# Gate and up products of six blocks by Strassen's scheme

## The chip, the cores and the metric

The kernel runs on one core of a Trainium2 chip. The metric is the device time of one execution in microseconds (us). Engine names: PE is TensorE (matmuls; PEld its weight loads), DVE is VectorE, ACT is ScalarE, POOL is GpSimd, SP is SyncE, which here only issues DMAs.

## The reference

`x` has 4 sequences of 1024 tokens with 512 channels, all in f32. One layer norm feeds two branches, and both are added to `x`:

```python
xn = _layernorm(x, axis=-1)
x = x + attn(xn, ...) + ffn(xn, w_gate, w_up, w_down)

def ffn(x, w_gate, w_up, w_down):
    gate = jnp.einsum('bsd,hd->bsh', x, w_gate)      # hidden width 2048
    up = jnp.einsum('bsd,hd->bsh', x, w_up)
    gated = jax.nn.silu(gate) * up
    return jnp.einsum('bsh,dh->bsd', gated, w_down)
```

The attention branch is an RMS norm, q, k and v by ternary weights, a causal linear attention with decay over chunks of 128 tokens (16 heads of 32, a running state `S` of 32x32 per head), two RMS norms and a ternary projection.

## The kernel before

The 4096 tokens are 8 blocks of 512. Every f32 operand of a large product is split into a high and a low f16 part, and a product is three matmuls: high by high, high by low, low by high. A matmul has a 128x128 weight tile and up to 512 moving columns.

**FFN.** `x` is normed and transposed into `xT` (high and low, 4 channel tiles of 128 rows, 512 token columns). The 2048 hidden units are 16 tiles `j`. For each `j`, `ffn_up` (L681) makes gate and then up: 4 channel tiles by 3 matmuls of 512 columns each, into one PSUM bank of the pool `ps_f` (3 banks). ACT applies Silu to gate (L693); DVE multiplies up by it and by a scale (L696); ACT casts to f16 (L699), and POOL or DVE subtracts for the low part (L700), giving `ghl`. Eight `j`s are a half `hh`; after them `ffn_down` (L704) makes the down products of four token chunks `k`, 24 matmuls each, and `add_acc` (L719) adds them to `acc`, which was loaded from `x`. Two `j`s share one scale, and are called a group or a pair.

The weights are scaled, split and stored to `gu_d` in DRAM while block 1 runs (`ffn0` with `stage`, `group_conv` L342). Later blocks load a 512 KB tile `gu` per `j` from there (L736; 4 buffers).

**Norm of the next block.** `ln_stats` computes mean and variance; `ln` (L430) splits four chunks of 128 tokens into high and low (ACT cast L436, POOL subtraction L437) and turns each by a DMA transpose into `xT` (L438).

**Attention.** `att_half` (L458) handles 256 tokens. It makes q and k (16 matmuls of 256 columns for each of four parts, tiles `wqkT` and `h`), sends them through DRAM (`sd`) into the layouts `qst` and `kst`, and turns k by a transpose into `kn`. Then follow v, and per chunk and quarter `qd` of the heads: `scores` (4 matmuls into the single bank of `ps_s`; DVE masks, L545; ACT casts, L547; POOL subtracts, L548), `intra` two steps later, `cross`, `state`, `norms`, and `proj`, which also ends in `add_acc`.

**Order.** `ffn0` and `ffn` are generators with 48 steps a block. After each step the main loop (L848 on) runs one step of the preparation `side` and `side2`, `make_h` (L444; the attention's own norm weight) where it is due, and one step of every attention half in flight. Halves start at steps 36 + 22.4 n (L841). PE keeps the program's order (`tc.keep_in_program_order`, L74); the order on the other engines and in SP's queue is set by the framework when the kernel is built. The attention's f32 temporaries and the FFN's share the tag `t32` (9 buffers of 512 columns).

## Time and profile before

Three runs took 1366.82, 1367.73 and 1367.89 us (median 1367.73). The profiled execution took 1368.61 us, of which 1366.7 are the span from the first to the last instruction.

| engine | busy us | share of the span |
|---|---|---|
| PE | 1322.6 | 97% |
| PEld | 695.6 | 51% |
| DVE | 719.9 | 53% |
| POOL | 619.6 | 45% |
| ACT | 550.3 | 40% |
| DMA queue of SP | | 47% of 16 engines |

In the profile, "psf<-xT,gu" means that the tile psf is written and xT and gu are read; "<-POOL gu L360" behind idle time names what ended it. A line number is that of the kernel; since every matmul is recorded by one helper, all matmuls have L74, and they are told apart by tiles. A PE row with 1.58 us and x13 is a run of thirteen matmuls; their modelled ends overlap the next run, so that a pitch is read from starts.

### The profile page before, as it was taken

The page shows a single profiled execution, that of the slowest core. Times are in us where ns is not written, and L with a number is a line of the kernel's source. Part 1 is how long each engine was busy: PE and PEld are TensorE (multiplying, and loading weights), DVE is VectorE, ACT ScalarE, POOL GpSimd, SP SyncE. Part 2 cuts the span into 40 slices and gives each one's busy share as a digit, 9 for nine tenths or more (in the row PEclk, how much of TensorE's full clock was granted, in tenths as well). Part 3 has the DMA queues.
Part 4 walks back from the last instruction along what each step waited for, and adds up shares of the span by engine and source line. Part 5 has one row for each costly group of instructions (what it writes and reads, how often), then busy time and mean ns, then how long its engine had stood idle before and what let it go on. Part 6 is the DMA issues. An engine that isn't in the chain of part 4 may idle for free.

```text
span 1366.7 us, 21760 instructions
## 1 busy us (share of the span) xinstructions
PE 1322.6 (97%) x8514; PEld 695.6 (51%) x8514; DVE 719.9 (53%) x1415; ACT 550.3 (40%) x1033; POOL 619.6 (45%) x603
## 2 busy tenths in 40 slices
PE   5998989999999999999999999999999999999998
PEld 2443445554555545455455545555555555565554
DVE  7897764445544354453644446453553445356444
ACT  6754443343433334333334243342424334244341
POOL 3657672444624254353634246342545245255451
PEclk9999999999999999999999999999999999999999
DMA  9833836146261554426363354626283444535420
GB/s 343 294 124 114 231 101 180 48 137 156 87 191 31 165 128 125 140 59 173 94 155 108 103 141 104 178 69 162 80 181 95 116 116 106 142 109 124 105 66 31
DMA packets 155974, 178.11 MB, mean 130 GB/s; under 512 B 101600, under 2 KB 101600, under 8 KB 155872
## 3 DMA queue, kind: packets, MB, share of 16 engines
q1 hardware_dynamic: 155728, 176.73, 47.0%
q8 instruction: 66, 1.08, 0.3%
q14 instruction: 36, 0.29, 0.1%
q10 hardware_dynamic: 144, 0.01, 0.0%
HBM read 119.55 MB, written 33.55 MB: 112 GB/s over the span
## 4 chain that ended last, share of the span: by engine, by line
PE 79%; DVE 7%; POOL 7%; issue 3%; DMA 3%; ACT 1%; SPq 0%; POOLq 0%; ACTq 0%; DVEq 0%
PE psf L74 58%; PE psa L74 19%; PE pss L74 2%; DMA xin<-in_x_dram 2%; DMA xT<-xn 1%; POOL t L548 1%; DVE acc L720 1%; POOL xn L437 1%; DVE t L696 1%; DVE gs L312 1%; POOL rs L396 1%; POOL wd L360 1%; DVE t L239 0%; POOL ghl L700 0%; POOL gu L360 0%
## 5 line engine op out<-in xcount | busy, mean ns | idle before, releaser
L74 PE MATMUL psf<-xT,gu 128*128 128x512 f16 x3072 | 703.4, 381 | 10.6 <-POOL gu L360 5.5
L74 PEld LDWEIGHTS <-gu 128*128 128x128 f16 x3072 | 294.7, 98 | 338.0 <-issue 10.1
L74 PE MATMUL psf<-wd,ghl 128*128 128x512 f16 x1536 | 352.3, 380 | 2.7 <-ACT t L693 1.1
L74 PEld LDWEIGHTS <-ghl 128*128 128x128 f16 x1536 | 146.9, 98 | 164.3 <-issue 3.3
L548 POOL TENSOR_TENSOR t<-t,t 128x512 f16<-128x512 f32 x128 | 149.5, 1168 | 164.2 <-ACT t L547 163.9
L700 POOL TENSOR_TENSOR ghl<-t,ghl 128x512 f16<-128x512 f32 x86 | 102.6, 1193 | 163.4 <-ACT ghl L699 150.2
L696 DVE SCALAR_TENSOR_TENSOR t<-psf,bsc,t 128x512 f32<-128x512 f32 x128 | 95.9, 749 | 121.2 <-PE psf L74 104.8
L699 ACT CAST ghl<-t 128x512 f16<-128x512 f32 x128 | 79.0, 617 | 176.1 <-DVE t L696 175.6
L545 DVE SCALAR_TENSOR_TENSOR t<-pss,rs,mask 128x512 f32<-128x512 f32 x128 | 95.3, 744 | 77.2 <-PE pss L74 74.7
L693 ACT ACTIVATE t<-psf,ug 128x512 f32<-128x512 f32 x128 | 87.5, 684 | 98.0 <-PE psf L74 96.6
L74 PE MATMUL psa<-h,wqkT 128*128 128x256 f16 x1024 | 122.2, 273 | 0.0
L519 POOL TENSOR_TENSOR t<-t,t 128x512 f16<-128x512 f32 x28 | 32.6, 1163 | 195.3 <-ACT t L518 195.3
L547 ACT CAST t<-t 128x512 f16<-128x512 f32 x128 | 79.1, 618 | 101.9 <-DVE t L545 96.3
L74 PEld LDWEIGHTS <-wqkT 128*128 128x128 f16 x1024 | 99.7, 98 | 23.4
L720 DVE SCALAR_TENSOR_TENSOR acc<-psf,c,acc 128x512 f32<-128x512 f32 x56 | 41.8, 747 | 63.0 <-PE psf L74 62.7
L74 PEld LDWEIGHTS <-t 128*128 128x128 f16 x1040 | 47.6, 97 | 35.0 <-POOL t L548 3.4
L74 PE MATMUL psa<-wvT,h 128*128 128x512 f16 x256 | 60.5, 379 | 0.0
L74 PE MATMUL pss<-qst,kst 96*128 96x128 f16 x512 | 49.2, 218 | 8.7 <-DVE t L545 6.5
L74 PE MATMUL psa<-wpT,vhl 128*128 128x512 f16 x240 | 56.7, 379 | 0.0
L620 POOL TENSOR_TENSOR vhl<-t,vhl 128x512 f16<-128x512 f32 x30 | 34.7, 1155 | 48.0 <-ACT vhl L619 48.0
L573 POOL TENSOR_TENSOR t<-t,t 128x512 f32<-128x512 f32 x28 | 36.1, 1288 | 44.1 <-DVE t L572 18.6
L508 DVE SCALAR_TENSOR_TENSOR vhl<-psa,rs,vhl 128x512 f16<-128x512 f32 x32 | 24.0, 749 | 56.2 <-ACT vhl L507 54.5
(188 smaller groups left out, 1340.8 us busy)
## 6 DMA issues: line engine op xcount, KB each, us to landing
gu<-gu_d SPq DMA_DIRECT2D x112, 512.0 KB, 3.6
qst<-sd SPq DMA_DIRECT2D x48, 256.0 KB, 4.8
kst<-sd SPq DMA_DIRECT2D x48, 256.0 KB, 4.7
xin<-in_x_dram SPq DMA_DIRECT2D x32, 256.0 KB, 3.0
acc<-in_x_dram SPq DMA_DIRECT2D x32, 256.0 KB, 2.8
gu_d<-gu SPq DMA_DIRECT2D x16, 512.0 KB, 4.1
sd<-qhl SPq DMA_DIRECT2D x16, 512.0 KB, 2.6
sd<-khl SPq DMA_DIRECT2D x16, 512.0 KB, 3.3
```

The lines of the kernel that those rows point to most:

```text
L74: tc.keep_in_program_order(nc.tensor.matmul(*a, **k))
L519: G.tensor_tensor(vrl, vr, vrh, ALU.subtract)
L545: V.scalar_tensor_tensor(sm, pss, u.rk, mask[:, 4 * qd : 4 * qd + 4, :], ALU.mult, ALU.mult)
L547: A.copy(u.smh, sm)
L548: G.tensor_tensor(u.sml, sm, u.smh, ALU.subtract)
L573: G.tensor_tensor(u.o, u.o, oc, ALU.add)
L620: G.tensor_tensor(on[:, 1, :], u.o3, on[:, 0, :], ALU.subtract)
L693: pa = A.activation(sl, pm, AF.Silu, scale=ug[:, j // 2 : j // 2 + 1])
L696: pv = V.scalar_tensor_tensor(gf, pm, bs[:, j // 2 : j // 2 + 1], sl, ALU.mult, ALU.mult)
L699: A.copy(ghl[:, 0, :], gf)
L700: E.tensor_tensor(ghl[:, 1, :], gf, ghl[:, 0, :], ALU.subtract)
L720: V.scalar_tensor_tensor(acc[g], ps, c, acc[g], ALU.mult, ALU.add)
```

## The change

Blocks 1 and 2 keep the plain products. In blocks 3 to 8 gate and up of one pair of hidden tiles are made together as a 2 by 2 block product in seven block products in place of eight (Winograd's form of Strassen's scheme). The two rows are up and gate; the two halves of the inner dimension are channels 0 to 255 and 256 to 511 (u1, u2, g1, g2); the two columns are the token halves of the block (x11, x21 for tokens 0 to 255; x12, x22 for the rest).

- Weight sums S1 = g1 + g2, S2 = S1 - u1, S3 = u1 - g1, S4 = u2 - S2 are made once by `comb`, in steps 50 to 86 (block 2), from weights that `load_comb` loads again, and stored to `gs_d`.
- Sums of x, T1 = x12 - x11, T2 = x22 - T1, T4 = x21 - T2, T3 = x22 - x12, are made by `ln` on POOL in the place of x's own rows, before the split and the transposes. There are seven split parts a block for four. `make_h` gets x12 back as T1 + x11.
- `Pair` makes the products p1 to p7. Each loads a 256 KB weight tile (`gu_tile`, 8 buffers) and has twelve matmuls of 256 columns (two hidden tiles by two channel tiles by three). p1, p6, p7 and p4 accumulate into one bank, which is read after p1, p6 and p7 as well; p5 and p3 share another; p2 has its own.
- `ffn` has again 48 steps a block. p4 and p3 of a pair stand behind p1 and p6 of the next. The down products of a half begin before the last pair's p4 and p3.

Besides: `XS` is 2^9 and not 2^10, and other scales follow; weights are stored by kind and channel half; q and k go to DRAM and to the transpose in quarters and not in halves (tag `qk`, 3 buffers); `acc` has 6 buffers and not 8, with its loads at steps 11 and 15 of a block; `t32` has 10; the projection weights are prepared right behind the qkv weights, one step of preparation for each step of the loop; `ln` runs over seven steps from the 40th of a block; `ln0` has copies of 256 columns in place of 512.

```diff
 RMS_EPS = 1.1920928955078125e-07
-XS = 2.0**10
+XS = 2.0**9
 QS = 2.0**-4
...
-    gu_d = dram.tile([P, NJ * 2048], F16, tag="gu_d", name="gu_d")
+
+
...
     def t32():
-        return wt([P, 512], F32, "t32", 9)
+        return wt([P, 512], F32, "t32", 10)
+    def gu_tile():
+        return wt([P, 2, 2, 2, P], F16, "gu", 8)
+
+    def xq_tile():
+        return wt([P, 2, 2, 2, UT], F16, "xq", 3)
...
 
-    HOLD = {"qst": (4, 1), "kst": (4, 1), "qhl": (2, 1), "khl": (2, 1)}
...
+    def load_comb(k):
+        g, r = divmod(k, 2)
+        for kind in range(2):
+            raw[g, kind, r] = t = wt([P, C], F32, *(("xin", 4) if k < 10 else ("xn2", 2)))
+            SY.dma_start(t, w_gu[2 * g + r, kind])
+
+    def comb(k):
+
+        g, r = divmod(k, 2)
+        sc = []
+        for kind in range(2):
+            src = raw.pop((g, kind, r))
+            A.activation(src, src, AF.Copy, scale=om[:, g, kind : kind + 1])
+            sc += [src[:, :256], src[:, 256:]]
+        g1, g2, u1, u2 = sc
+        ta, tb = t32(), t32()
+        G.tensor_tensor(ta[:, :256], g1, g2, ALU.add)
+        G.tensor_tensor(ta[:, 256:], ta[:, :256], u1, ALU.subtract)
+        G.tensor_tensor(tb[:, :256], u1, g1, ALU.subtract)
+        G.tensor_tensor(tb[:, 256:], u2, ta[:, 256:], ALU.subtract)
+        st = xq_tile().rearrange("p a b c t -> p (a b c t)").rearrange("p (s n q) -> p s n q", s=4, n=2)
+        for n, t in enumerate((ta, tb)):
+            tv, sn = t.rearrange("p (a q) -> p a q", a=2), st[:, 2 * n : 2 * n + 2]
+            A.copy(sn[:, :, 0], tv)
+            V.tensor_tensor(sn[:, :, 1], tv, sn[:, :, 0], ALU.subtract)
+        SY.dma_start(gs_d[:, g, :, r], st.rearrange("p s n q -> p s (n q)"))
 
...
+    def staged(src):
+
+        xn2 = wt([P, 2, 2, UT], F16, "xn2", 2)
+        A.copy(xn2[:, :, 0], src)
+        G.tensor_tensor(xn2[:, :, 1], src, xn2[:, :, 0], ALU.subtract)
+        return xn2
...
     def ln(b):
         rs, xts = lnst.pop(b)
-        xT = wt([P, 2, CC, HB], F16, "xT", 1)
-        blk[b] = [xT, None, rs]
-        for k in range(4):
-            xn2 = wt([P, 2 * C], F16, "xn2", 2).rearrange("p (a c) -> p a c", a=2)
-            A.copy(xn2[:, 0, :], xts[k])
-            G.tensor_tensor(xn2[:, 1, :], xts[k], xn2[:, 0, :], ALU.subtract)
-            SY.dma_start_transpose(
-                xT[:, :, :, k * P : (k + 1) * P].rearrange("p a c t -> p (a c) t"),
-                xn2.rearrange("p a c -> p (a c)"),
+        xq = [None] * 7
+        blk[b] = [xq, None, rs]
+
+        def unit(tile, src, k):
+            xn2 = staged(src)
+            turned(
+                tile[:, :, :, :, k * P : (k + 1) * P].rearrange("p s n c t -> p (s n c) t"),
+                xn2.rearrange("p s n c -> p (s n c)"),
             )
-            yield
+
+        def pair(tiles, qs):
+            t = xq_tile()
+            xq[qs[0]], xq[qs[1]] = t[:, 0], t[:, 1]
+            for k in range(2):
+                unit(t, tiles[k].rearrange("p (s c) -> p s c", s=2), k)
+                yield
+
+        xa, xb = xts[:2], xts[2:]
+        yield from pair(xa, (X11, X21))
+        t2 = t32().rearrange("p (k c) -> p k c", k=2)
+        for k in range(2):
+            T1, x21, x12, x22 = xa[k][:, :256], xa[k][:, 256:], xb[k][:, :256], xb[k][:, 256:]
+            G.tensor_tensor(T1, x12, T1, ALU.subtract)
+            G.tensor_tensor(t2[:, k], x22, T1, ALU.subtract)
+            G.tensor_tensor(x21, x21, t2[:, k], ALU.subtract)
+            G.tensor_tensor(x12, x22, x12, ALU.subtract)
+        tq = wt([P, 2, 2, 2, P], F16, "xq2", 1)
+        xq[XT2] = tq.rearrange("p k n c t -> p n c k t")
+        xn2 = staged(t2)
+        turned(tq.rearrange("p k n c t -> p (k n c) t"), xn2.rearrange("p k n c -> p (k n c)"))
+        yield
+        yield from pair(xa, (XT1, XT4))
+        yield from pair(xb, (XT3, X22))
 
     def make_h(b, half):
 
-        xT = blk[b][0]
+        xs = blk[b][0]
         hsl = slice(half * UT, (half + 1) * UT)
         h = wt([P, 2, CC, UT], F16, "h", 1)
         blk[b][1] = h
         for cp in range(0, CC, 2):
             th = t32().rearrange("p (c t) -> p c t", c=2)
-            G.tensor_tensor(th, xT[:, 0, cp : cp + 2, hsl], xT[:, 1, cp : cp + 2, hsl], ALU.add)
+            if b < 2:
+                xa = xs[cp // 2][:, :, :, hsl]
+            else:
+                xa = xs[((X11, X21), (XT1, X22))[half][cp // 2]]
+            G.tensor_tensor(th, xa[:, 0], xa[:, 1], ALU.add)
+            if b > 1 and half and cp == 0:
+                for n in range(2):
+                    G.tensor_tensor(th, th, xs[X11][:, n], ALU.add)
...
+        kn = wt([P, 2, 2, 2, 2, P], F16, "kn", 1)
         for i in range(4):
-            dhi, dlo = (qhi, qlo) if i < 2 else (khi, klo)
-            pair = slice(2 * (i % 2), 2 * (i % 2) + 2)
+            p = i % 2
+            hl = wt([P, 2, 2, UT], F16, "qk", 3)
             pq = bank(ps_a, (P, 2, UT))
             for n in range(2):
                 w = slice((2 * i + n) * P, (2 * i + n + 1) * P)
                 for c in range(CC):
                     T.matmul(pq[:, n, :], wqkT[:, c, w], hhi[:, c, :], start=(c == 0), stop=False)
                     T.matmul(pq[:, n, :], wqkT[:, c, w], hlo[:, c, :], start=False, stop=(c == CC - 1))
-            A.activation(dhi[:, pair, :], pq, AF.Copy, scale=QS)
-            V.scalar_tensor_tensor(dlo[:, pair, :], pq, QS, dhi[:, pair, :], ALU.mult, ALU.subtract)
-            if i % 2 == 1:
-                src, dst, sel = (qhl, qst, (0, 1, 0)) if i == 1 else (khl, kst, (0, 0, 1))
-                sd = dram.tile([P, 2 * CC * UT], F16, tag=f"sd{i}", name=nm("sd"), bufs=2)
-                SY.dma_start(sd, src.rearrange("p a c t -> p (a c t)"))
-                sv = sd.rearrange("(h d) f -> d h f", d=D)
+            A.activation(hl[:, 0], pq, AF.Copy, scale=QS)
+            V.scalar_tensor_tensor(hl[:, 1], pq, QS, hl[:, 0], ALU.mult, ALU.subtract)
+            if p == 0:
+                sd = dram.tile([P, 2, 2, 2 * UT], F16, tag=f"sd{i}", name=nm("sd"), bufs=2)
+            SY.dma_start(sd[:, :, p], hl.rearrange("p a c t -> p a (c t)"))
+            if i > 1:
+                SY.dma_start_transpose(
+                    kn[:, p].rearrange("p a c k q -> p (a c k) q"), hl.rearrange("p a c t -> p (a c t)")
+                )
+            if p == 1:
+                dst, sel = (qst, (0, 1, 0)) if i == 1 else (kst, (0, 0, 1))
+                sv = sd.rearrange("(h d) a c t -> d h a (c t)", d=D)
                 for g in range(3):
-                    SY.dma_start(
-                        dst[D * g : D * g + D].rearrange("p h c t -> p h (c t)"),
-                        sv[:, :, sel[g] * CC * UT : (sel[g] + 1) * CC * UT],
-                    )
-                if i == 3:
-                    SY.dma_start_transpose(
-                        kn.rearrange("p a c k q -> p (a c k) q"), khl.rearrange("p a c t -> p (a c t)")
-                    )
+                    SY.dma_start(dst[D * g : D * g + D].rearrange("p h c t -> p h (c t)"), sv[:, :, sel[g]])
             yield
 
         vs, vrs = [], []
...
-    def load_acc(b):
-        for k in range(4):
-            acc[4 * b + k] = load_x(4 * b + k, "acc", 8)
+    def load_acc(b, ks=range(4)):
+        for k in ks:
+            acc[4 * b + k] = load_x(4 * b + k, "acc", 6)
             parts[4 * b + k] = 1 + (2 if b else NG)
 
...
+
+
+
+        def __init__(self, b, p, last):
+            self.xq, self.p, self.last = blk[b][0], p, last
+            self.ug, self.bs = ug[:, p : p + 1], bsc[:, p : p + 1]
+            self.g = [wt([P, 2, 2, 256], F16, "ghl", 8) for _ in range(2)]
+
+        def prod(self, ps, src, q, first, last):
+            w = gu_tile().rearrange("p a b c d -> p (a b c d)")
+            SY.dma_start(w, src.rearrange("p r f -> p (r f)"))
+            w = w.rearrange("p (r n c q) -> p r n c q", r=2, n=2, c=2)
+            x = self.xq[q]
+            for r in range(2):
+                o = ps[:, r * 256 : (r + 1) * 256]
+                if q == XT2:
+                    o = o.rearrange("p (k t) -> p k t", k=2)
+                for c in range(2):
+                    T.matmul(o, w[:, r, 0, c], x[:, 0, c], start=(first and r + c == 0), stop=False, skip_group_check=True)
+                    T.matmul(o, w[:, r, 0, c], x[:, 1, c], start=False, stop=False, skip_group_check=True)
+                    T.matmul(o, w[:, r, 1, c], x[:, 0, c], start=False, stop=(last and r + c == 2), skip_group_check=True)
+
+        def p1(self):
+            self.a, self.up = bank(ps_f), [t32(), t32()]
+            self.prod(self.a, gu_d[:, self.p, 1, 0], X11, True, False)
+            A.activation(self.up[0], self.a, AF.Copy, scale=self.bs)
+
+        def p6(self):
+            self.prod(self.a, gs_d[:, self.p, 1], XT2, False, False)
+            A.activation(self.up[1], self.a, AF.Copy, scale=self.bs)
+
+        def p5(self):
+            self.d = bank(ps_f)
+            self.prod(self.d, gs_d[:, self.p, 0], XT1, True, False)
+
+        def p2(self):
+            ps = bank(ps_f)
+            self.prod(ps, gu_d[:, self.p, 1, 1], X21, True, True)
+            V.scalar_tensor_tensor(self.up[0], ps, self.bs, self.up[0], ALU.mult, ALU.add)
+
+        def p7(self):
+            self.prod(self.a, gs_d[:, self.p, 2], XT3, False, False)
+            self.sl = t32()
+            A.copy(self.sl, self.a)
+            V.tensor_tensor(self.sl, self.d, self.sl, ALU.add)
+            A.activation(self.sl, self.sl, AF.Silu, scale=self.ug)
+
+        def p4(self):
+            self.prod(self.a, gu_d[:, self.p, 0, 1], XT4, False, True)
+            sl = t32()
+            A.activation(sl, self.a, AF.Silu, scale=self.ug)
+            self.gated(0, sl, V if self.last else G)
+
+        def p3(self):
+            self.prod(self.d, gs_d[:, self.p, 3], X22, False, True)
+            V.scalar_tensor_tensor(self.up[1], self.d, self.bs, self.up[1], ALU.mult, ALU.add)
+            self.gated(1, self.sl, V)
+
+        def gated(self, h, sl, E):
+            gf, gt = self.up[h], self.g[h].rearrange("p n r q -> p n (r q)")
+            E.tensor_tensor(gf, gf, sl, ALU.mult)
+            A.copy(gt[:, 0], gf)
+            (V if self.last else G).tensor_tensor(gt[:, 1], gf, gt[:, 0], ALU.subtract)
+
+    def ffn(b):
+        for hh in range(2):
+            old, gts, pds = None, [], {}
+
+            def down(k, ns):
+                if k not in pds:
+                    pds[k] = bank(ps_f)
+                pd, ksl = pds[k], slice(k % 2 * P, k % 2 * P + P)
+                for n in ns:
+                    gt, w = gts[n // 2][k // 2], wd[:, 8 * hh + n]
+                    gh, gl = gt[:, 0, n % 2, ksl], gt[:, 1, n % 2, ksl]
+                    T.matmul(pd, gh, w[:, 0, :], start=(n == 0), stop=False)
+                    T.matmul(pd, gh, w[:, 1, :], start=False, stop=False)
+                    T.matmul(pd, gl, w[:, 0, :], start=False, stop=(n == 7))
+                if n == 7:
+                    add_acc(b * 4 + k, pd, c2[:, hh : hh + 1])
+
+            for p in range(4 * hh, 4 * hh + 4):
+                new = Pair(b, p, p % 4 == 3)
+                new.p1()
+                yield
+                if old:
+                    old.p4()
+                new.p6()
+                yield
+                if old:
+                    old.p3()
+                new.p5()
+                yield
+                new.p2()
+                new.p7()
+                gts.append(new.g)
+                if p == 2:
+                    load_acc(b, (0, 1))
+                if p == 3:
+                    load_acc(b, (2, 3))
+                old = new
+                yield
+            down(0, range(4))
+            yield
+            down(0, range(4, 6))
+            old.p4()
+            yield
+            old.p3()
+            down(1, range(3))
+            yield
+            down(1, range(3, 6))
+            down(0, range(6, 8))
+            yield
+            down(1, range(6, 8))
+            down(2, range(3))
+            yield
+            down(2, range(3, 8))
+            yield
+            down(3, range(4))
+            yield
+            down(3, range(4, 8))
+            yield
 
...
     def prep():
-        qw = load_rows(qkv_w, ("qst", "kst", "qhl", "khl"))
+        qw = load_rows(qkv_w, ("qst", "kst", "h", "qk", "qk"))
         SY.dma_start(nw_bc, norm_w.partition_broadcast(P))
+        yield
         yield from prep_qkv_w(qw)
-
-    def prep_proj():
-        pw = [wt([P, C], F32, "acc", 8) for _ in range(4)]
-        for r in range(4):
-            SY.dma_start(pw[r], proj_w[r * P : (r + 1) * P, :])
-        yield
+        pw = load_rows(proj_w, ("qst",))
...
@@ -860,6 +1070,12 @@
             for hf in list(halves):
                 if next(hf, 1) == 1:
                     halves.remove(hf)
+            for k in range(2 * NG):
+                tk = 50 + round(2.4 * k)
+                if t == tk - 2:
+                    load_comb(k)
+                if t == tk:
+                    comb(k)
             t += 1
             if t == 6 * NG - 6:
                 SY.dma_start(pnw_bc, proj_nw.partition_broadcast(P))
@@ -867,8 +1083,8 @@
                 if i == TS - (22 if b else 15):
                     ln_stats(b + 1)
                 if i == TS - (9 if b else 5):
-                    lns = ln(b + 1)
-                if i in ((TS - 8, TS - 7, TS - 5, TS - 4) if b else range(TS - 4, TS)):
+                    lns = ln(b + 1) if b else ln1()
+                if b == 0 and i >= TS - 4 or b and i >= TS - 9:
                     next(lns, 1)
         for _ in lns:
             pass
```

## The prediction

> **What bounds the kernel now.** I read the busy times first, then the chain that ended last, then TensorE (PE) stretch by stretch, and last the waits of the DMA queue.
>
> ```profile
> PE 1322.6 (97%) x8514; PEld 695.6 (51%) x8514; DVE 719.9 (53%) x1415; ACT 550.3 (40%) x1033; POOL 619.6 (45%) x603
> PE 79%; DVE 7%; POOL 7%; issue 3%; DMA 3%; ACT 1%; SPq 0%; POOLq 0%; ACTq 0%; DVEq 0%
> L74 PE MATMUL psf<-xT,gu 128*128 128x512 f16 x3072 | 703.4, 381 | 10.6 <-POOL gu L360 5.5
> L74 PE MATMUL psa<-h,wqkT 128*128 128x256 f16 x1024 | 122.2, 273 | 0.0
> ```
>
> PE carries 79% of the chain, and gate and up products (psf<-xT,gu) are half of its busy time. No other engine is busy for more than 53%. By stretch (columns: length, then busy time and count of PE, weight loads, DVE, ACT and POOL, then granted clock, DMA share, GB/s):
>
> ```profile
> 340.00:500.00 160.00, 157.85 (x1042) 83.40 (x1040) 71.53 (x139) 58.69 (x110) 66.08 (x63) 1.00 0.46 126
> 500.00:660.00 160.00, 157.53 (x1042) 83.78 (x1042) 79.82 (x154) 62.77 (x114) 70.08 (x70) 1.00 0.43 116
> 660.00:820.00 160.00, 157.75 (x1031) 83.06 (x1029) 75.79 (x143) 58.85 (x107) 68.52 (x68) 0.99 0.45 121
> 820.00:980.00 160.00, 159.29 (x1054) 84.16 (x1053) 77.43 (x149) 60.47 (x111) 71.51 (x71) 1.00 0.47 123
> 980.00:1140.00 160.00, 160.00 (x1062) 84.58 (x1058) 73.47 (x146) 61.13 (x114) 70.06 (x70) 1.00 0.47 119
> 500.00:520.00 20.00, 17.53 (x126) 9.10 (x126) 14.10 (x34) 7.17 (x15) 13.31 (x17) 1.00 0.10 27
> ```
>
> The middle of the kernel has PE busy for all but 7.6 of 800 us. So fewer matmul columns there shorten the kernel one for one until another wait appears. The last line shows what such a wait looks like: with POOL busy for 67% and DVE for 71% of a 20 us stretch, PE lost 2.5 us.
>
> **The product saving.** Matmul durations overlap, so I take the pitch from starts in the timeline:
>
> ```profile
> 699.76 1.58 PE L74 MATMUL psa<-h,wqkT 128*128 128x256 f16 x13
> 701.18 2.75 PE L74 MATMUL psf<-xT,gu 128*128 128x512 f16 x12
> 703.77 1.89 PE L74 MATMUL psa<-wpT,vhl 128*128 128x512 f16 x8
> 705.50 1.91 PE L74 MATMUL psa<-h,wqkT 128*128 128x256 f16 x16
> 707.25 2.75 PE L74 MATMUL psf<-xT,gu 128*128 128x512 f16 x12
> ```
>
> Twelve 512-column matmuls take 703.77 - 701.18 = 2.59 us, 0.216 each; sixteen 256-column ones take 707.25 - 705.50 = 1.75 us, 0.1093 each. A pair of hidden tiles costs 4 x 12 x 0.216 = 10.37 us before. After, seven products of twelve 256-column matmuls cost 84 x 0.1093 = 9.18 us. The 48 pairs of blocks 3 to 8 give 48 x 1.19 = **-57 us**. Down products keep their count and width.
>
> A weight load stands before every matmul, and there are now 84 loads of 98 ns a pair for 48. [...] Here all loads use the full array; were they serial, a pair would cost 84 x (98 + 109) = 17.4 us for 48 x (98 + 216) = 15.1, a loss of about 110 us. The wqkT row denies it: at 0.1093 us a matmul the 98 ns load is hidden already.
>
> **What the other engines get, per block of 8 pairs.** ACT: a pair now has two scaled copies out of PSUM, one plain copy, two Silus and two casts, for two Silus and two casts. At 0.68 (Silu from PSUM), 0.58 (plain copy from PSUM) and 0.62 (cast) that is 4.54 for 2.60 us, +15.5 a block; three more casts in ln add 1.9. DVE: a pair has two scaled adds (0.75), one add from PSUM (0.685) and one product of two SBUF tiles (0.85, as L700 on DVE), 3.03 us; the last pair of each half has two products and two subtractions, 5.6. Mean 3.67 for 2.14, +12. POOL: six pairs with one product (1.29) and two subtractions (1.19), 22.0 for 11.9; ln has three more subtractions (3.5) and eight sums of 256 columns, for which there is no row: half of a 1.29 sum is 0.64, the whole is the upper end, I take 0.7, 5.6 in all; make_h has two more sums of 1.17. Together +21.4. In the 960 us from 340 to 1300 the mean loads were DVE 77.4, ACT 61.0 and POOL 69.4 per 160 us. A block is some 163 us (step 3.4), so after the change, in 154 us: DVE (79 + 12) / 154 = 59%, ACT 52%, **POOL (71 + 21) / 154 = 60%**. None is a bound by its sum; what counts is latency.
>
> [...]
>
> **Where latency comes back to PE.**
>
> ```profile
> 643.38 0.39 PE L74 MATMUL pss<-qst,kst 96*128 96x128 f16 x4
> 644.32 0.74 DVE L545 SCALAR_TENSOR_TENSOR t<-pss,rs,mask 128x512 f32<-128x512 f32 x1
> 645.79 1.16 POOL L548 TENSOR_TENSOR t<-t,t 128x512 f16<-128x512 f32 x1 [1.70 <-ACT t L547]
> 646.46 0.69 ACT L693 ACTIVATE t<-psf,ug 128x512 f32<-128x512 f32 x1 [0.75 <-PE psf L74]
> ```
>
> (a) p6 accumulates into the bank that p1's ACT copy must have read. By the last line and its matmuls (first start 643.61, next slot 646.20), ACT ends 0.95 us after the next matmul could start. In six of eight pairs old.p4 (1.31 us) covers that; the first pair of a half has only attention work (about 0.8 us a step). 12 places at 0 to 1.0 us; I take 0.3, **+3.6**. Behind p6 waits everything in PE's fixed order. (b) Scores have one bank, released by DVE at 645.06, 1.68 us after 643.38. A step that holds only p1 brings the next scores after about 0.2 + 1.31 + 0.2 = 1.7 us: no slack where DVE has another 0.75 us operation first. The banks that p1 and p2 need are freed the same way behind one product (1.31 + 0.8 us against 0.26 + 0.75). I take 1 us a block, **+6**. (c) Scores reach intra through DVE, ACT and POOL: 3.57 us (643.38 to 646.95). Two steps later it is needed: 5.85 us before, 1.31 + 2.62 + 0.84 = 4.8 us where one step is p1's. One POOL operation ahead (1.2 us) uses that up, and ln puts 15 POOL operations in seven steps. I take 1.2 us a block, **+7**. For (a) to (c) together the low end is -6 (most of today's idle goes, as in 980 to 1140); the high end is the 12% of the 500 to 520 stretch over a third of each block: 154 / 3 x 0.12 x 6 = +37.
>
> **Block 2, weight sums.** Sixteen times: two scalings (0.71), two casts (0.62), four POOL sums (0.7), two DVE subtractions (0.85), two 256 KB loads, one 512 KB store, every 2.4 steps or 8.2 us. POOL gets 34% more on its 46%, ACT 32% on 39%. PE's own work there is unchanged. 0 if all fits, 16 times one POOL burst less the cover, about 1 us, at the high end; I take **+5**. If that cover fails, the scores of both halves in flight are late.
>
> **Start.** ln0's copies are split in two (four more ACT and four more DVE operations of some 0.4 us, less what each saves), and projection weights are prepared before step 36 and not after: some 10 us of DVE work goes into 80 to 110 us, where DVE was busy for 95%. Against that, mask and proj work leaves 105 to 165 us, where PE once waited 5.0 us for POOL. -4 to +8; I take **+2**.
>
> **Queues.** Weight loads go from 16 of 512 KB to 56 of 256 KB a block; SP spends about 0.33 us on each, 18.5 for 5.3 us, and with transposes and stores about 50 of 154 us. Bytes rise by 38 MB for weights and 17 MB for the sums on 178 MB; transposes by a fifth. The DMA share would go from 47% to some 65%. Costed at 0: cover is the eight tiles ahead. Six acc tiles for eight: the second two of a block are loaded at its step 15, when the block before has freed two by its projections (steps 58 + 44.8b and 62 + 44.8b of the whole, 103 and 107 for a load at 111): 0, cover four steps. In block 2 the load at step 61 may hold SP one step for the tile freed at 62, under four j's of weights.
>
> Sum: -57 + 3.6 + 6 + 7 + 5 + 2 = -33 us. The profiled execution took 1368.61 us (span 1366.7 and 1.9 around it): 1335.2. It lies 0.9 above the median of 1367.73, so **1335** to the nearest us.
>
> **Rivals.**
> *All hidden.* POOL at 10.0 of 10 us (110 to 120) once cost PE nothing. Only (a) is left: about 1315. 15%.
> *POOL and DVE second.* The 37 of the high end, 10 in block 2 and 2 at the start: -8, 1360. For it: 500 to 520, and t32 tiles (a pair holds its sums over six steps, ten buffers for all). Against: most stretches run at 45% without loss. 18%.
> *Weights late.* A tile freed by product n is needed at n + 8: seven products and attention, 9.18 + 4 x 0.8 = 12.4 us, less 3.6 to land, 8.8 us of slack; it was 3 x 6.8 - 3.6 = 16.8. SP works in order, and a load stands behind stores that wait:
>
> ```profile
> SPq L484 <- DVE qhl L480: 56.5, 13, 13.2
> gu<-gu_d SPq DMA_DIRECT2D x112, 512.0 KB, 3.6
> ```
>
> The longest such wait, 13.2 us, would make a product 4.4 us late; two a block cost 12 x 4.4 = 53: 1335 + 53 = **1388**, slower. It decides from 33 / 12 = 2.75 us each. Against: the mean wait is 4.3 us, and no PE wait on gu loads shows today. 11%.
> *Narrow products cost more than 0.109.* At the 119.3 ns of the busy column a pair saves 0.35, 17 in all: 1375. Break-even with the other terms is at 117. Against: the starts above. 4%.
> Forecast (1320 to 1350): 52%.
>
> **How the numbers follow.** About 0.2% (2.7 us) is what a measurement can tell from no change. Faster: 52 + 15 + 15 of the 18 = 82%; same 4%; slower 14%. The range 1312 to 1362 leaves out the slower cases and the tails of the first two rivals.
>
> **What would show it.** Right: 256-column products at 9.2 us a pair with DVE, ACT and POOL near 60, 52 and 60% in the middle, PE idle below 5 us in 154. Wrong: PE waits on DMA gu (weights late), on POOL L548's successor or on t32 releases (POOL second), or a 256-column pitch above 0.117.

## The result, and the profile after

Four runs after took 1429.73 to 1435.54 us (median 1430.82), four before 1366.82 to 1368.62 (1367.81): a ratio of 1.0468, 95% interval 1.0443 to 1.0492. The change makes the kernel 4.7% slower. The forecast was 1335. The profiled execution took 1435.54 us, with a span of 1433.3.

First the page of the changed kernel, with the same rows as before, and its DMA queue:

```profile
PE 1298.0 (91%) x10242; PEld 875.4 (61%) x10242; DVE 861.1 (60%) x1547; ACT 676.5 (47%) x1263; POOL 816.5 (57%) x793
q1 hardware_dynamic: 248560, 236.00, 60.0%
PE 52%; DVE 13%; POOL 11%; DMA 11%; ACT 6%; issue 4%; SPq 2%; POOLq 0%; DVEq 0%; ACTq 0%
L74 PE MATMUL psf<-xq,gu 128*128 128x256 f16 (+1 forms) x4800 | 671.0, 296 | 64.1 <-ACT t L861 31.8
```

PE has fallen from 79% of the chain to 52%, and DVE, POOL and DMA took its place. No engine other than PE is near full: their busy shares are near those forecast. The gate and up products now follow 64.1 us of idle time (10.6 before), half of it ended by ACT at L861. That is the copy of p1's result.

I split the trace where a block's first gate or up product starts: once around block 2, once around blocks 3 to 8. Columns as in the stretches of the prediction, first before:

```profile
178.90:346.90 168.00, 165.17 (x1093) 87.59 (x1094) 87.23 (x164) 65.03 (x119) 78.28 (x81) 1.00 0.45 123
346.90:1366.70 1019.80, 1007.55 (x6695) 535.21 (x6692) 489.52 (x938) 383.77 (x707) 432.72 (x418) 1.00 0.44 116
```

and after:

```profile
179.20:380.10 200.90, 173.71 (x1096) 88.89 (x1094) 119.31 (x190) 99.46 (x181) 135.57 (x146) 0.96 0.65 184
380.10:1433.30 1053.20, 975.48 (x8423) 714.06 (x8420) 602.14 (x1045) 473.65 (x869) 574.80 (x544) 0.98 0.58 154
```

- Start: 178.9 to 179.2, +0.3 us.
- Block 2: 168.0 to 200.9, **+32.9**. Idle PE (length less busy) grew from 2.8 to 27.2. PE's busy time grew by 8.5 at about the same count of matmuls, so those ran slower (clock 0.96).
- Blocks 3 to 8: 1019.8 to 1053.2, **+33.4** where -57 was worked out for the products. Idle PE grew from 12.3 to 77.7, +65.5. PE's busy time fell by 32.1 and not by 57. Of the 25 us between, some 20 are the lower clock (0.98 against 1.00): with four things left out, below, the same matmuls took 955.6 us at 1.00. The other 5 are, by that run, saving that did not come.

-57 + 65.5 + 25 + 32.9 + 0.3 = +66.7, the difference of the spans (66.6). Which instructions PE waited for, in the view of its waits (us in total, times, longest wait in us):

```profile
PE psf L74 <- ACT t L861: 31.8, 11, 8.0
PE pss L74 <- DVE t L635: 14.0, 10, 5.2
PE psf L74 <- ACT t L783: 11.4, 4, 5.7
...
PE psf L74 <- ACT t L879: 7.9, 2, 4.6
...
PE psf L74 <- DMA gu<-gs_d: 2.4, 1, 2.4
```

L635 masks scores, L783 is Silu in blocks 1 and 2, L879 the copy of p7's result. Eleven waits for one kind of copy are the largest entry. The weights that the scheme loads from gs_d were late once.

**Anatomy of one wait**, from the timeline (start, duration, engine, instruction; in brackets the idle time before and what ended it):

```profile
469.58 1.47 PE L74 MATMUL psf<-xq,gu 128*128 128x256 f16 x12
...
470.93 1.27 POOL L663 TENSOR_TENSOR t<-t,t 128x512 f32<-128x512 f32 x1 [1.53 <-DVE t L653]
...
472.22 0.63 ACT L690 ACTIVATE junk<-t 128x512 f16<-128x512 f32 x1 [0.55 <-POOL t L663]
472.27 1.26 POOL L692 TENSOR_TENSOR t<-t,nw_bc 128x512 f32<-128x512 f32 x1
...
473.56 0.63 ACT L693 ACTIVATE junk<-t 128x512 f16<-128x512 f32 x1 [0.62 <-POOL t L692]
...
474.19 0.67 ACT L861 ACTIVATE t<-psf,bsc 128x512 f32<-128x512 f32 x1
...
474.91 2.71 PE L74 MATMUL psf<-xq,gu 128*128 128x256 f16 x12 [3.65 <-ACT t L861]
...
477.43 1.27 PE L74 MATMUL psa<-t,kn 128*128 128x128 f16 x12
```

p1's twelve matmuls begin at 469.58 and at 0.109 us each are done by 470.9. The copy needs 0.67 us and begins at 474.19, since two squares of the attention's norm (L690, L693) stand ahead of it in ACT's queue, and each of them waits for a POOL operation (L663, L692). ACT itself is idle for part of that time. PE, which works in the program's order, has p6 next and stands for 3.65 us. Then p6's twelve matmuls take until the next run starts at 477.43, 2.5 us for 1.31, at a granted clock of 0.50 (475 to 478 us): the wait is paid for twice.

The longest wait has another thing ahead of the copy. ACT, then PE:

```profile
1081.64 0.62 ACT L473 CAST xn<-xin 128x512 f16<-128x512 f32 x1 [13.53 <-DVE xin L441]
...
1085.29 0.62 ACT L608 CAST t<-t 128x512 f16<-128x512 f32 x1 [1.93 <-DVE t L604]
...
1086.39 0.68 ACT L861 ACTIVATE t<-psf,bsc 128x512 f32<-128x512 f32 x1
...
1077.68 1.47 PE L74 MATMUL psf<-xq,gu 128*128 128x256 f16 x12
1087.12 5.28 PE L74 MATMUL psf<-xq,gu 128*128 128x256 f16 x24 [7.97 <-ACT t L861]
```

L473 casts the *next* block's x. In the program it belongs some 39 steps behind this copy; in the order that the framework planned it stands ahead. It is held back by the norm of that x on DVE (L441), which needs x's statistics, which wait for the loads of x. Between that cast and the copy ACT waits once more, 1.93 us for DVE (L608).

### The profile page after: what moved, and what is told of

Its sections match the earlier page's. It is cut to its first block, busy times and chain, and to the rows that moved or that the text cites. A ratio compares the mean times of both kernels' runs of the same rounds, so it can differ in the third digit from the quotient of the medians.

```text
span 1433.3 us, 26577 instructions
## 1 busy us (share of the span) xinstructions
PE 1298.0 (91%) x10242; PEld 875.4 (61%) x10242; DVE 861.1 (60%) x1547; ACT 676.5 (47%) x1263; POOL 816.5 (57%) x793
## 3 DMA queue, kind: packets, MB, share of 16 engines
q8 instruction: 80, 1.31, 0.4%
## 4 chain that ended last, share of the span: by engine, by line
PE 52%; DVE 13%; POOL 11%; DMA 11%; ACT 6%; issue 4%; SPq 2%; POOLq 0%; DVEq 0%; ACTq 0%
PE psf L74 38%; PE psa L74 13%; DMA sd<-qk 2%; DMA xin<-in_x_dram 2%; DVE h L552 2%; DMA xin<-in_w_gu_dram 2%; POOL t L638 2%; PE pss L74 1%; POOL xn L474 1%; DVE acc L810 1%; DMA xn<-in_w_gu_dram 1%; DMA xq<-xn 1%; DVE t L635 1%; DVE xq L401 1%; POOL t L692 1%
## 5 line engine op out<-in xcount | busy, mean ns | idle before, releaser
L74 PE MATMUL psf<-xq,gu 128*128 128x256 f16 (+1 forms) x4800 | 671.0, 296 | 64.1 <-ACT t L861 31.8
L74 PEld LDWEIGHTS <-gu 128*128 128x128 f16 x4800 | 471.9, 100 | 216.2 <-issue 70.8
L638 POOL TENSOR_TENSOR t<-t,t 128x512 f16<-128x512 f32 x128 | 150.9, 1180 | 131.1 <-ACT t L637 130.6
L635 DVE SCALAR_TENSOR_TENSOR t<-pss,rs,mask 128x512 f32<-128x512 f32 x128 | 95.3, 745 | 89.4 <-PE pss L74 89.0
L898 POOL TENSOR_TENSOR ghl<-t,ghl 128x512 f16<-128x512 f32 x72 | 90.4, 1262 | 34.2 <-ACT ghl L897 34.2
L897 ACT CAST ghl<-t 128x512 f16<-128x512 f32 x96 | 59.0, 617 | 75.0 <-DVE t L896 67.2
L572 DVE SCALAR_TENSOR_TENSOR qk<-psa,qk 128x512 f16<-128x512 f32 x64 | 43.9, 689 | 79.7 <-ACT qk L571 74.6
L896 POOL TENSOR_TENSOR t<-t,t 128x512 f32<-128x512 f32 x36 | 46.4, 1288 | 54.5 <-ACT t L886 54.4
L896 DVE TENSOR_TENSOR t<-t,t 128x512 f32<-128x512 f32 x60 | 62.8, 1046 | 8.5 <-ACT t L886 6.6
L474 POOL TENSOR_TENSOR xn<-xin,xn 128x512 f16<-128x512 f32 x40 | 48.2, 1208 | 26.3 <-ACT xn L473 26.0
L571 ACT ACTIVATE qk<-psa 128x512 f16<-128x512 f32 x64 | 37.7, 591 | 50.4 <-PE psa L74 49.3
L552 DVE SCALAR_TENSOR_TENSOR h<-t,nwT,h 128x256 f16<-128x256 f32 x64 | 51.9, 849 | 15.2 <-ACT h L551 15.1
```

The source lines that it names most:

```text
L74: tc.keep_in_program_order(nc.tensor.matmul(*a, **k))
L474: G.tensor_tensor(xn2[:, :, 1], src, xn2[:, :, 0], ALU.subtract)
L552: V.scalar_tensor_tensor(h[:, 1, c, :], th[:, n, :], nwT[:, c : c + 1], h[:, 0, c, :], ALU.mult, ALU.subtract)
L571: A.activation(hl[:, 0], pq, AF.Copy, scale=QS)
L572: V.scalar_tensor_tensor(hl[:, 1], pq, QS, hl[:, 0], ALU.mult, ALU.subtract)
L635: V.scalar_tensor_tensor(sm, pss, u.rk, mask[:, 4 * qd : 4 * qd + 4, :], ALU.mult, ALU.mult)
```

## The experiments

Each is one run (the kernel before, run beside them, took 1367.9 to 1369.8). The four runs of the changed kernel lie up to 5.8 us apart, so a single step of that size is not told from none. Differences of the time are from the median, 1430.8, or from the version that a run builds on. "Blocks 3 to 8" is the length from block 3's first gate product to the end, 1053.2 after and 1019.8 before; block 2 is 200.9 after. These lengths are of the profiled execution, the slowest of the four, so a gain read from them can be up to 5 us too large. The texts set in front of each result name the runs by the labels in brackets. Of the theories that they speak of, A is that the reads of product banks in the middle of a pair set the loss, A2 that late POOL work reaches those reads through ACT's queue, B that transfers are late, and C that POOL's added work sets the loss.

**Out: the reads of the product banks** (e1_no_read).

```diff
-            A.activation(self.up[0], self.a, AF.Copy, scale=self.bs)
+            A.activation(v3(self.up[0]), mask[:, :4, :], AF.Copy, scale=self.bs)
```

(so too for p6's and p7's copy)

> The copies of p1 (L861), p6 (L865) and p7 (L879) read an SBUF tile and not the product bank, so up and gate are not the reference's; same count and kind of ACT instructions. Theory A (products that accumulate into a bank which ACT must have read make PE wait at the end of ACT's in-order queue): the waits of PE on L861 and L879 (31.8 + 7.9 us) go, and with them a like share of the slow-clock time behind them (26 us over some 65 us of extra idle, so about 16): 1431 - 55 = about 1376. Rival B (transfers are late, DMA 60% busy): PE waits the same time elsewhere, 1415 to 1431. Rival C (POOL and DVE near 60% delay scores, intra and down): the waits move there, 1400 to 1420.

1411.72, blocks 3 to 8 1035.3: -19 from the change, and not the -55 of A. All L861 waits are gone, and others grew:

```profile
PE psf L74 <- DVE t L874: 12.2, 12, 2.1
PE psa L74 <- DMA vhl<-vhl: 12.2, 4, 4.7
```

So the reads themselves are worth 19 us, though PE's waits on the three copies came to some 40: what delays the copies delays others too.

**Out: the weight sums of block 2** (e2_no_sums). `comb` and `load_comb` are not called, and p6, p5, p7, p3 take weights from gu_d.

> Leaves out the weight sums and their loads and stores in block 2; the products of blocks 3 to 8 load plain weights of the same size in their place. All theories: block 2 falls from 200.9 to about the 168 us it took before, 1431 - 33 = 1398. If the sums only filled time that other waits would take, it stays above 1415.

1395.40; block 2 took 166.7, blocks 3 to 8 1052. The sums cost the whole of block 2's loss, and nothing behind it.

**Order: the casts of the next x behind the pair's last Silu** (e3_ln_behind).

```diff
-            xn2 = staged(src)
+            with after(lastev):
+                xn2 = staged(src)
```

> Only the order on ACT changes: the casts of the next block's x (L473) may not stand ahead of the last pair's Silu of the block. Theory A with the planned order as its cause (17 of these casts stand within six places ahead of an L861 or L865 of the block before): the PE waits of 8.0, 5.6, 4.6 and 3.2 us shrink to about 1 each, -17 us idle and about -8 of slow clock: 1405. Rival B: no change, or slower, as the transposes start later: 1425 to 1440. Rival C: 1425 to 1435.

1423.45: only -7, little more than the runs differ by, and 26.4 us of waits for p1's copy stay. The early casts alone are not it.

**Order: p4 and p3 of the pair before, both between p1 and p6** (e4_later_p6).

> p4 and p3 of the old pair both stand between p1 and p6 (and p5, p2 in a half's first pair), so that the copy of p1 has two products and two steps' attention, some 4 us, in place of 2. Theory A: each wait on L861 shrinks by some 2 us, 31.8 to about 13, and the slow clock with it: 1431 - 27 = 1404. Rival B: 1425 to 1435. Rival C: 1420 to 1435, as the masks of old pairs come no sooner.

1437.71: none of the 27 us that A forecast. The waits for p1's copy (L861) fell, but less work was left between p6 and p7, and p7 must wait for p6's copy (L865):

```profile
PE psf L74 <- ACT t L865: 28.7, 12, 5.5
...
PE psf L74 <- ACT t L861: 8.9, 3, 4.0
```

**Out: weight loads** (e5_one_load). One load per pair in place of seven (288 of 336 gone; all products of a pair use the same weights).

> The seven products of a pair share one weight load, so gate and up are not the reference's; 288 of 336 weight loads of blocks 3 to 8 and 75 MB are gone, engines and PE keep their instructions. Rival B (transfers late): most of the 65 us of added idle and 26 us of slow clock in these blocks goes, 1431 - 60 = 1370 or below. Theory A (in-order queues of ACT and DVE, whatever the transfers): the waits on L861 behind norms and state stay, only the 8.0 us one behind late x goes with its slow clock: 1415 to 1431. Rival C (POOL and DVE load): 1420 to 1431.

1421.97, blocks 3 to 8 1045.6. The waits for p1's copy stand at 31.6 us as before: the weight loads are worth some 8 us there.

**Out: POOL's added work** (e6_less_pool; the sums of x, make_h's two more sums, the first half's gating product, the gates' low part in all but the last pair of a half).

> Leaves out the POOL work that the scheme added: x's sums, the two more sums of make_h, and for pairs that are not the last of a half the gating product of the first token half and both low parts, so its output is not the reference's. POOL falls by 30 us a block, below what it had before. Rival C: waits on scores, intra, down and the norms chain shrink, and with them those behind it on ACT: 1431 - 50 = 1380. Theory A in its narrow form (planned order on ACT): L861 still waits behind norms and state, 1410 to 1425. Rival B: 1425 to 1435.

1399.07, blocks 3 to 8 1021.7: -31, between what C (1380) and A (1410 to 1425) forecast. The waits for p1's copy fell from 31.8 to 15.2: part of what holds them is POOL. The run takes out more than was added: POOL's busy time in these blocks went from 574.8 to 392.2 us, and was 432.7 before.

**Out: the two squares of the norms on ACT** (e7_no_squares; a constant in their place).

> Leaves out the two sums of squares of norms on ACT (L690, L693; a constant stands for them, so the attention's scale is not the reference's); POOL and DVE work of norms stays. Theory A: what stood ahead of L861 at 475, 488, 567, 738, 1299 and 1393 us were these two, waiting for POOL; some 15 of 31.8 us of L861 waits go and 7 of slow clock: 1408. Rival B: 1425 to 1435. Rival C: POOL unchanged, 1420 to 1431.

1398.34, blocks 3 to 8 1022.5: -31, more than expected; the waits for p1's copy fell from 31.8 to 16.8. ACT loses 1.6 us of work per pair of squares, and two waits for POOL ahead of the copies; the norms behind the squares can also start sooner. This run doesn't part the three; the run on order alone, below, does in part.

**Plain products in all blocks, the rest of the change kept** (e8_plain; order, quarters of q and k, scales, start; no sums).

> Undoes the scheme alone: plain gate and up products in all blocks, no weight sums, no sums of x; the quarters of q and k, the weight layout, the buffers and the preparation stay as changed. All theories that lay the loss to the scheme: 1368, within 8. If the other parts cost time: above 1380.

1366.65. So the scheme and its sums hold all of the loss.

**The four things out together** (e9_all_out; bank reads, sums, POOL's work, squares).

> All that e1, e2, e6 and e7 take out, taken out together; the output is not the reference's. If these four hold the whole loss, PE is bound by its matmuls again: 1368 - 57 = 1311, at most 1325. If something else is left (weight loads, short steps, DVE): 1340 or more, and the waits that are left name it.

1327.69. From block 3 on:

```profile
342.90:1325.90 983.00, 955.57 (x8423) 705.37 (x8420) 562.67 (x1046) 431.07 (x752) 380.19 (x368) 1.00 0.62 164
```

The same matmuls as after, at a clock of 1.00: 955.6 us busy, where 1007.6 - 57 = 950.6 was worked out. The saving of the scheme is real, some 52 us of PE's time. The time lies between the two forecasts (1325 and 1340): 27.4 us of idle PE are left in these blocks, for 12.3 before. Together the four take 103 us off the change; one by one 19, 35, 32 and 32, 118, so that they overlap a little.

**The copies of p1 and p6 on DVE** (e10_copies_dve).

```diff
-            A.activation(self.up[0], self.a, AF.Copy, scale=self.bs)
+            V.tensor_scalar(self.up[0], self.a, self.bs, None, ALU.mult)
```

> Computes the reference. As the changed kernel, but p1 and p6 are copied from the product bank by DVE and not by ACT. If ACT's queue decides (what stands ahead of the copies there waits for POOL): L861's waits shrink by more than DVE's grow, 1412. If any in-order queue with such work is as bad: 1425 to 1440, with the waits on DVE.

1460.10. The wait moved and doubled:

```profile
PE psf L74 <- DVE t L861: 66.3, 18, 10.7
```

So it is not ACT alone: on DVE, too, what stands ahead of the copy holds PE. DVE is also the busier engine of the two (663.6 us in blocks 3 to 8 with the copies), and this run doesn't part the one from the other.

**Order alone, nothing left out.** The squares one step later and behind the products' copies (f2_norms):

```diff
+            with after(pin):
+                A.activation(junk, o, AF.Square, accum_out=sq[:, 0:1])
+                A.activation(junk, o2, AF.Square, accum_out=sq[:, 1:2])
```

> Computes the reference. Of f1_all's edits only the squares: one step later and behind the product copies. Theory A2: most of e7's 33 us, 1405. If e7's gain came from less ACT work: 1425 to 1435.

1413.40, -17: about half of what leaving the squares out gave, with the same work on every engine. The waits for p1's copy fell from 31.8 to 22.5. The sums' ACT and DVE operations behind Silu and gating (f3_sums_pin):

> Computes the reference. Only the scalings and casts of the weight sums may not stand ahead of the last Silu and gating product of block 2. Theory A2: block 2's waits on L783 (5.7), L786 (3.8) and part of the down and score waits go, -12: 1419. If block 2 loses by engine load alone: no change, 1428 to 1433.

1426.54, -4, within what runs differ by; block 2 took 197.5. Both, with the casts of x and the states' copies treated alike and the sums' loads a step earlier (f1_all):

> Computes the reference. The two squares of norms are issued one step later, and they, the copies of the state, the casts of the next block's x and the scalings and casts of the weight sums may not stand ahead of the product copies issued before them; sums' weights are loaded three steps ahead and not two. Theory A2 (POOL is late by some us, what waits for it stands ahead of a product copy on ACT, PE waits behind that, and the clock falls): the squares and casts ahead of product copies go from 21 to 8 places, so about as much as in e7 (1398) and some of block 2's 33 us: 1385. If e7's gain came from less ACT work and not from the order: 1420 to 1435.

1413.70: no better than the squares alone, where 1385 was forecast. That version with x's statistics behind DVE's reads of the product banks as well (g1_stats_pin):

```diff
-                V.bn_stats(st, xt)
-                V.bn_aggr(mv[:, k, :], st)
+            with after(pin if b else []):
+                V.bn_stats(st, xt)
+                V.bn_aggr(mv[:, k, :], st)
```

> Computes the reference. f1_all, and the statistics of the next block's x may not stand ahead of DVE's evictions issued before them. If the 7.5 us wait of f1_all at 1067 us (DVE behind statistics whose x is late) is the planned order: 1404. If it is the transfers: 1410 to 1415.

1394.36, -19; the waits for p1's copy are down from 14.9 to 7.8 us. That, with the first half's gating product and x's sums on DVE and not on POOL (g3_pool_to_dve):

> Computes the reference. g1_stats_pin, and the gating product of the first token half and x's sums go from POOL to DVE: POOL falls by some 13 us a block, to about 51%, DVE rises by some 9, to 65%. If POOL's load holds back the norms chain: 1390. If DVE's load is as bad: 1400 to 1415.

1381.93, -12, blocks 3 to 8 1017.0. With the loads of x in SP's queue behind the weight load before them (g6_x_late):

> As g3_pool_to_dve, but the loads of the next block's x may not stand in SP's queue ahead of the weight load issued just before them in the program; nothing is left out. If the x loads that are put ahead push back transposes and weight loads, the 6.4 us wait of PE for kst near 1042 us goes and blocks 3 to 8 fall by some 8 us, the time to 1374. If the order in SP's queue is not what holds the blocks, the time stays within 4 us of 1382.

1379.34, blocks 3 to 8 1013.6. The waits for kst fell from 7.1 to 3.8 us in all, the time by 2.6, less than runs differ by: the order in SP's queue isn't shown to hold the blocks. This is the fastest that leaves nothing out, and still some 10 us slower than before.

**Block 2**, on the version of 1381.93. One scale for gate and up, so that the sums need no scaling on ACT (g4_one_scale):

> Computes the reference. g3_pool_to_dve, with one common scale for gate and up of a pair, so that the sums need no scaling by ACT: two ACT operations fewer for each of the sixteen sums, and ACT waits for no load. If block 2 loses by ACT's waits for loads: block 2 falls by 15, 15 below g3_pool_to_dve. If by POOL's sums: at most 5 below it.

1393.28: block 2 took 190.7 as before (190.6), and the start grew by 12 us. The four sums on DVE (g5_sums_dve):

> As g3_pool_to_dve, and the four sums of each weight tile in block 2 are made on DVE and not on POOL; nothing is left out. If POOL's share of the weight sums is what holds block 2 (190.6 us in g3_pool_to_dve against 166.7 us without sums), block 2 falls by some 10 us to 180 and the time from 1382 to 1372. If the sums hold any in-order queue in which they stand, block 2 stays at 185 to 200 and the time at 1377 to 1392.

1386.88: block 2 took 193.7. POOL was busy for 84.7 us of it in place of 131.7 and DVE for 139.2 in place of 119.9, and it gained nothing.

Neither run takes the sums' transfers out. In block 2 of the changed kernel ACT, which scales the raw weights (L389), waited for their loads more than for anything else:

```profile
ACT xin L389 <- DMA xin<-in_w_gu_dram: 24.9, 14, 6.6
ACT xn L389 <- DMA xn<-in_w_gu_dram: 16.7, 7, 5.2
```

With one scale it waited there for the stores of the sums, whose buffers its casts need:

```profile
ACT xq L409 <- DMA gs_d<-xq: 28.3, 7, 8.1
```

## Why the prediction was wrong

**Right.** *The product saving of 57 us.* The pitch stands in the timeline after:

```profile
823.25 1.47 PE L74 MATMUL psf<-xq,gu 128*128 128x256 f16 x12
824.56 1.69 PE L74 MATMUL psa<-h,wqkT 128*128 128x256 f16 x14
```

Twelve in 1.31 us, 0.109 each; the rival of narrow products that cost more falls. *Queues at 0:* right within 8 us (one load per pair); the rival of late weights falls with one wait of 2.4 us. *Start +2:* +0.3 (DVE was busy for 27.1 of the 30 us from 80 to 110, 90% and not 95%), though in the runs above that change nothing there the start took from 173.9 to 180.1 us. *Engine sums:* over blocks 3 to 8 DVE 57%, ACT 45%, POOL 55%, for 59, 52 and 60 in the forecast; none is a bound by its sum. That the shares agree is in part luck: a block took 175.5 us and not 154, and DVE 100 us of it and not 91 (its gating products took 1.05 us each, priced at 0.85).

**Wrong: the price of (a), the copy of p1.** The latency terms (a) to (c) were +17 us, and at most +37. Measured: +65.5 us of idle PE and some 20 of slower clock. The waits of blocks 3 to 8, before:

```profile
PE pss L74 <- DVE t L545: 3.7, 4, 1.2
...
PE psa L74 <- POOL t L548: 0.6, 1, 0.6
```

and after (the rows of L861 and L879 are those shown above):

```profile
PE psa L74 <- POOL t L638: 8.1, 8, 2.5
...
PE psf L74 <- DVE t L874: 5.2, 5, 1.7
PE pss L74 <- DVE t L635: 5.0, 6, 1.4
```

Terms (b) (the masks, now L635, and DVE's read of p2's bank, L874) and (c) (POOL's low part of the scores, now L638) came out near their 6 and 7 us. Term (a) was 31.8 for 3.6, and the wait of p4 for p7's copy (L879, 7.9 us) was no term. Place and mechanism of (a) were named: p6 behind the ACT copy of p1, and all of PE's order behind p6. Its price failed. I took the copy's delay from one row of a trace in which ACT was free when the product ended (0.95 us), counted only the first pair of a half as uncovered, and allowed 0 to 1.0 us. Seven of the eleven waits, 22.4 us, are at such first pairs, but last up to 8.0 us; the other four, 9.5 us, come though p4 of the pair before stands between. The price of such a copy is what may stand *ahead* of it in the queue of the engine that reads, and what that waits for. Squares out -31, POOL's work out -31, and order alone (squares later on ACT -17, then statistics later on DVE -19) show it; how the 31 us of each run split between shorter waits ahead of the copies and less work is not shown. The rival "POOL and DVE second" was the nearest in kind, but it too took its price from busy shares and its sign was wrong: 1360.

**Wrong: the clock behind each wait.** It was no term at all. The trace of before had the row, and I passed over it:

```profile
125.26 4.26 PE L74 MATMUL psf<-xT,gu 128*128 128x512 f16 x10 [5.03 <-POOL gu L360]
```

Ten matmuls took until 129.36, 4.1 us, where ten pitches are 2.16, at a granted clock of 0.50 (125 to 129 us): this wait of 5.03 us cost 7.

**Wrong: block 2**, +5 (0 to 16). Measured +32.9, and without the sums -34 from the change. I added POOL's sums to its busy share and asked whether they fit. They fit (135.6 of 200.9 us), and PE still stood for 27.2 us in place of 2.8, most of it for masks (L635, 7.4 us), the casts of the gated product (L789, 6.2) and Silu (L783, 5.7), which share their queues with the sums. That the sums hold these queues up is argued, not shown; that the sums with their loads and stores cause the loss is shown by the run without them.

**Open.** Why block 2 still takes some 24 us more than without sums (190.6 against 166.7) in the version of 1381.93: it is not the scaling on ACT, nor POOL as the place of the sums; order pins took 3 to 9 us. The sums' loads and stores, for which ACT waits, are a rival that no run tested alone. Pins also make the framework plan the whole order anew, so single steps of a few us may be due to that. Other orders of p1 to p7, or a spare PSUM bank for p1, weren't tried.

## What to carry to other kernels

Here a product that had to be read before the next one could start put the reading engine's queue on PE's path: 31.8 us of PE's waits with p1's copy on ACT, which was busy for 45% of blocks 3 to 8, and 66.3 us with it on DVE (p6's copy moved there too). Price such a read by what the planned order may put ahead of it and by what those instructions wait for, not by the engine's busy share. Splitting a long accumulation into short ones that are read in between spent slack that no busy column showed. To PE's waits add what the clock loses behind them: here 1.2 us in the run behind a wait of 3.65 us, some 2.5 behind one of 7.97, nothing behind one of 2.74.

## What the runs showed of the hardware

How long a wait must be to lower PE's clock isn't sharp in this case. In the timeline after:

```profile
487.82 2.03 PE L74 MATMUL psf<-xq,gu 128*128 128x256 f16 x12 [2.17 <-ACT t L861]
489.64 3.06 PE L74 MATMUL psa<-wpT,vhl 128*128 128x512 f16 x8
492.53 2.78 PE L74 MATMUL psf<-xq,gu 128*128 128x256 f16 x24
...
738.04 2.72 PE L74 MATMUL psf<-xq,gu 128*128 128x256 f16 x12 [3.15 <-ACT t L861]
...
1204.91 1.47 PE L74 MATMUL psf<-xq,gu 128*128 128x256 f16 x12 [1.60 <-ACT t L861]
...
1298.82 1.47 PE L74 MATMUL psf<-xq,gu 128*128 128x256 f16 x12 [2.74 <-ACT t L861]
```

1.47 us is a run of twelve at a granted clock of 1.00 (1203 to 1206 us), 2.72 one at 0.50 (738 to 740 us). Waits of 1.60 and 2.74 us cost nothing, one of 3.15 nearly a whole run (2.51 us from start to start, for 1.31). The one of 2.17 us cost 0.5 us in its own run (1.82 us from start to start, for 1.31) and 1.2 in the next: eight matmuls of 512 columns took 2.89 us, where eight pitches are 1.73. The granted clock was 1.00 up to 488.4 us, 0.6 us into the first of the two runs, and 0.50 from 488.6 to 491 us. So the slow time began after this wait was over. After 7.97 us a run of 24 took 5.28, where one at a clock of 1.00 shows 2.78 (the row at 492.53): there the clock was 0.50 from 1083 us on, while PE still stood, and up to 1092.4 us, so that the slow time lasted some 5 us behind the wait. What sets it off is not shown: a wait of 2.17 us had slow time behind it, and one of 2.74 us had none.
